# Window attention and AFNO over eight images: input and output turned by VectorE, the setup's loads and the plan's objective rewritten

## The chip, the cores and the metric

The kernel runs on one core of one Trainium2 chip. The core has TensorE (PE, with its weight loads listed apart as PEld), VectorE (DVE), ScalarE (ACT), GpSimd (POOL) and SyncE (SP), which here issues nearly all DMA transfers. The metric is the device time of one execution in microseconds (us); the number for the kernel before is the median of three runs. Everything is computed in float32, apart from one small bias product in bfloat16.

## The reference, cut

Two layers, one after the other, on an input of 8 images x 192 channels x 64 x 64. Layer 0 is window attention with the 16 largest scores kept in each row, and an MLP. Layer 1 is an AFNO (a Fourier transform, a tiny MLP on every frequency, the inverse transform) and an MLP.

```python
def _L0_conv_ref(x, ...):
    b, c, h, w = x.shape
    xs = jnp.transpose(x.reshape(b, c, h * w), (0, 2, 1))
    shortcut = _layer_norm(xs, norm1_g, norm1_b)
    ...
    qkv = (xin @ qkv_w.T + qkv_b).reshape(B_, N, 3, HEADS, HEAD_DIM)
    ...
    attn = jnp.einsum('bhnd,bhmd->bhnm', _l2n(q), _l2n(k)) * temperature
    kth = jax.lax.top_k(attn, IN_CC)[0][..., -1:]
    attn = jnp.where(attn >= kth, attn, NEG)
    rpb = jnp.transpose(rpb_table[REL_IDX], (2, 0, 1))
    attn = jax.nn.softmax(attn + rpb[None], axis=-1)
    out = jnp.einsum('bhnm,bhmd->bhnd', attn, v)
    ...
    out = out @ proj_w.T + proj_b
    ...
    x2 = shortcut + out
    hdn = _layer_norm(x2, norm2_g, norm2_b)
    hdn = jax.nn.gelu(hdn @ fc1_w.T + fc1_b, approximate=False) @ fc2_w.T + fc2_b
    x2 = x2 + hdn
    return jnp.transpose(x2, (0, 2, 1)).reshape(b, c, h, w)

def _L1_conv_ref(x, ...):
    skip1 = x
    xn = _layernorm(x.transpose(0, 2, 3, 1), n1_g, n1_b).transpose(0, 3, 1, 2)
    x = skip1 + _afno(xn, fc1_w, fc1_b, fc2_w, fc2_b)
    x_perm = x.transpose(0, 2, 3, 1)
    xn2 = _layernorm(x_perm, n2_g, n2_b)
    h = jax.nn.gelu(xn2 @ mlp1_w.T + mlp1_b, approximate=False) @ mlp2_w.T + mlp2_b
    return (h + x_perm).transpose(0, 3, 1, 2)
```

Here 192 channels, 6 heads of 32, MLPs of width 768. Both layers want tokens on the partitions for the norms and channels on the partitions for the products, so data is turned several times.

## The kernel before, in words

An image is cut into 8 bands of 8 rows (512 tokens, one row of windows), 64 bands in all. The work is written as generators, one for each task: `front(b, i)` loads and turns a band of image b, normalizes it and computes q, k and v; `attention(b, i, hb)` does half a band's windows; `back(b, i)` the projection and layer 0's MLP; `forward`, `pointwise` and `inverse` do the AFNO of an image in 12 groups of 16 channels; `leave(b, j)` does layer 1's MLP for a band and writes it out. AFNO needs all 8 bands of its image, so image b's AFNO and `leave` run beside attention of image b+1. Image 0 has nothing beside it, and image 7's last stages neither.

Before each piece of work a generator yields `op(engine, weight, ...)`: the engine (or a choice of two), an estimate of its time in units of about 10 ns, the buffers it takes and gives back (`get`, `put`), and what it waits for (`after`). `listed` (L96) collects these, and `Plan` (L130) plays them against each other: `run` (L215) places the ready piece that can begin first on an engine, ties decided by a key with the task's place in the program (`self.place`, 360 units an image); a buffer given back is free 15 units later (L268). `search` (L278) tries 80 noisy orders of the next 4000 units, keeps the one with the most work placed (PE's counts in full, other engines' 0.15), follows it for 2000 units and repeats. The kernel is then issued in that order, so every engine has a fixed instruction order. A piece on SP is a group of DMA issues, which SP works off in that order too, waiting at each for what it needs.

The parts that the change touches:

- Input. `load_band` (L377) brings a band in three transfers, channels on the partitions: 128 channels in rows of 2048 bytes (L381) and twice 64 channels in rows of 1024 bytes (L384). `front` turns it with six PE transposes into PSUM tile `lt` (L880, L884), ACT or DVE copies that to `xt` (L889). `loading` (L864) loads two bands ahead.
- Output. `leave` adds MLP and residual into `zt` (DVE, L1479), turns it with six PE transposes into `pz` (L1487), adds the MLP's second bias on ACT while it moves `pz` to `z` (L1491), and stores `z` with three transfers (L1494, L1496). `zt` is in an `xa` buffer, `z` in an `hn` buffer.
- The turn that other parts have already. In `mlp` with `by_dma` (L751) DVE turns blocks of 32 x 32 (L756, tile `lt_b` or `lt_d`, in an `att` buffer), four transfers write the blocks to DRAM rows (L765), three bring them back as channels (L768, L770, tile `hn_b` or `hn_d`). Attention's probabilities go likewise from image 1 on (`tt`, `ar`, `at`; L1069, L1078, L1081).
- Setup. `setup_layer1` (L606) loads AFNO's constants in one piece with the weight 0. Layer 1's gain `n1g` comes in eight transfers of single floats (L640), the MLP's weights `wmlp` right after it (L675). `setup_rows` (L518) spreads three vectors over the partitions through the tile `wides`.
- In attention each pair of rows of the top-16 search uses two of four `s2` buffers (L1138).

Of the kernel before, what the change touches and what calls it, by code (L numbers as in the profile page):

```python
# [9 lines left out]
FP = mybir.dt.float32  # L10
# [6 lines left out]
C = 192  # L17
# [112 lines left out]
class Plan:  # L130
# [84 lines left out]
    def run(self, until, noise=None):  # L215
        ops, clock, mode, units = self.ops, self.clock, self.mode, self.units
        at, front, place, ready = self.at, self.front, self.place, self.ready
        while ready:
# [48 lines left out]
            for name in put:  # L267
                units[name].append(end + (150 if engine == "sp" else 15))  # L268
                units[name].sort()
# [8 lines left out]
    def search(self, tries=80, step=2000, horizon=4000, spread=25):  # L278
        draw = random.Random(1)
        now = 0  # L280
        while self.ready:
            now = max(now, self.clock["pe"])
            kept, best = self.save(), None
            for k in range(tries):
                seed = draw.random()
                noise = drawn(seed, spread) if k else None
                if not self.run(now + horizon, noise):
                    self.restore(kept)
                    continue
                worth = 0  # L290
                for _, _, engine, begin, weight in self.log[kept[-1]:]:
                    part = min(weight, max(0, now + horizon - begin))
                    worth += part if engine == "pe" else 0.15 * part
                if not self.ready:
                    worth = 1e9 - max(self.clock.values())
                if best is None or worth > best[0]:
                    best = worth, seed if k else None
                self.restore(kept)
            seed = best[1]
            self.run(now + step, drawn(seed, spread) if seed is not None else None)  # L300
            now += step
        return [(self.names[task], engine, number) for number, task, engine, _, _ in self.log]

# [38 lines left out]
def program(ctx, tc, x, out, w):  # L342
# [34 lines left out]
    def load_band(b, i):  # L377
        xin = strip("xin", 2, f"xin_{b}_{i}")
        rows = x[b, :, 8 * i : 8 * i + 8, :]
        xa = xin[:, :BAND].rearrange("p (r s) -> p r s", s=HW)  # L380
        nc.sync.dma_start(xa, rows[0:CA])  # L381
        for t in range(2):
            xb = xin[64 * t : 64 * t + 64, BAND:ROW].rearrange("p (r s) -> p r s", s=HW)
            nc.sync.dma_start(xb, rows[CA:C, 4 * t : 4 * t + 4, :])  # L384
        xins[b, i] = xin

# [67 lines left out]
    wides = spare("wides", [128, 3, 2, 128])  # L454
# [20 lines left out]
    alongs = {name: ctile(name, [128, 2 * C]) for name in ("gain1", "bias1", "bias2")}  # L475
    gain1, bias1, bias2 = (
# [41 lines left out]
    def setup_rows():  # L518
# [17 lines left out]
        vectors = (vec(G1), pbias, vec(FC2B))  # L536
        yield op("dve", 150)
        for wide, v in zip((wides[:, i] for i in range(3)), vectors):
            for k, n in enumerate((CA, 64)):
                nc.vector.tensor_copy(wide[0:n, k, :], v[k][0:n].to_broadcast([n, 128]))  # L540
        yield op("pe", 60, "full", get="ps", put="h")
        pt = psum("along")
        for i in range(3):
            for k, n in enumerate((CA, 64)):
                to = pt[:, i // 2, i % 2 * C + k * CA : i % 2 * C + k * CA + n]
                nc.tensor.transpose(to, wides[0:n, i, k, :], ident[0:n, 0:n])
# [59 lines left out]
    def setup_layer1():  # L606
        yield op("pool", 0, get="xf", after=[("att", 0, 0, 1)])
# [9 lines left out]

# [3 lines left out]
        for k in range(4):  # L621
            src = w["fwd2"].rearrange("(a b k e) v -> k b a e v", a=2, k=4, e=2)[k]
            nc.sync.dma_start(frow[8 * k : 8 * k + 8], src)
        for c in range(1, 4):
            nc.sync.dma_start(frow[32 * c : 32 * c + 32], frow[0:32])
        inv1 = sb.tile([128, 128], FP, tag="xf", name="inv1", bufs=1)
# [6 lines left out]
        n1t = w["n1"]  # L633
        for c in range(2):
            for k in range(4):
                src = bass.AP(
                    n1t.tensor, n1t.offset + c * 2 * HC + k, [[0, 32], [4, 24], [1, 1]]
                )
                dst = n1g[32 * k : 32 * k + 32, 24 * c : 24 * c + 24]
                nc.sync.dma_start(dst.unsqueeze(2), src)  # L640
            nc.sync.dma_start(n1b2[:, c, :], w["n1"][c : c + 1, 1, :])
        yield op("dve", 120, after=[("att", 0, 1, 1)])
# [31 lines left out]
        nc.vector.tensor_scalar(n1b2, n1b2, float(HW), None, ALU.mult)  # L674
        wmlp.extend(load_mlp("wmlp1", "wmlp2"))  # L675
# [66 lines left out]

    def mlp(src, nm, w1, fc1_bias, w2, by_dma, then=None):
# [7 lines left out]
        if by_dma:  # L751
            ready = yield op("dve", 101, get="att rows", put="xa", after=last)
            turned = sb.tile([128, 6, 2, 2, 32], FP, tag="att", name=f"lt_{nm}", bufs=ATT_BUFS)
            whole = to.rearrange("p j (g k) -> p j g k", k=32)
            for t, g, c, n in ((0, 0, 0, 6), (1, 6, 4, 2), (1, 8, 0, 4)):
                nc.vector.transpose(  # L756
                    turned[:, c : c + n, t].rearrange("p g j k -> p j g k"),
                    whole[:, :, g : g + n],
                )
# [103 lines left out]

    def loading(b, i):  # L864
        yield op("sp", 154, get="xin", after=[], done=("xin", b, i))
        load_band(b, i)
# [3 lines left out]
    def front(b, i):  # L870
# [3 lines left out]
        yield op("pe", 66, "full", get="ps xt", put="xin", after=loaded)  # L874
        xin = xins.pop((b, i))
        pt = psum(f"lt_{nm}")
        for t, j in PAIRS:
            q = 2 * t + j
            c0 = t * (64 + C)
            nc.tensor.transpose(  # L880
                pt[:, j, c0 : c0 + CA], xin[:, q * 128 : (q + 1) * 128], ident
            )
        for j in range(2):
            nc.tensor.transpose(  # L884
                pt[:, j, CA : CA + 128], xin[:, BAND + j * 128 : BAND + (j + 1) * 128], ident
            )
        done = yield op(EITHER, (69, 87), put="ps")
        xt, pair = tokens("xt", XT_BUFS, f"xt_{nm}")
        copy(done, xt, pt[:, :, : 2 * C])  # L889
# [79 lines left out]
        def by_block(half, p):  # L969

            return half.rearrange("c (n b) -> c b n", b=2)[:, p]

        def qk_a(pq, p, first):
            for t in range(2):
                tok = by_block(xn[:, t * HALF : (t + 1) * HALF], p)
# [9 lines left out]
        def qk_b(pq, p, first):  # L985
            flags = dict(skip_group_check=True, stop=not first)
            for t in range(2):
                rows = slice(64 * t, 64 * t + 64)
                tok = by_block(xn[rows, BAND:ROW], p)
                nc.tensor.matmul(  # L990
                    pq[:, t, : 2 * C], tok, wqkv[1][rows, : 2 * C], start=first, **flags
                )
# [97 lines left out]
    def attention(b, i, hb):  # L1090
# [41 lines left out]
        for k0 in range(0, 12, 2):  # L1132
            yield op("dve", 90, get="sm" if k0 == 0 else "")
            if k0 == 0:
# [3 lines left out]
                sb.tile([128, 64], FP, tag="s2", name=f"s2_{nm}_{k0 + k}", bufs=4) for k in range(2)  # L1138
# [323 lines left out]
    def leave(b, j):  # L1462
# [3 lines left out]
        if j == 0:  # L1466
# [5 lines left out]
        xy = xys[b][0]  # L1472
        acc, last = yield from mlp(
            lambda t, q: xy[:, t, q, j, :], f"d{nm}", wmlp[0], fcb[:, 1, :], wmlp[1], True
        )
        left[b] -= 1
        yield op("dve", 88, get="xa", put="ps xy" if left[b] == 0 else "ps")
# [6 lines left out]
        )  # L1484
        yield op("pe", 66, "full", get="ps hn", put="xa")
# [29 lines left out]
        ([(setup_mlp(1, lambda: wmlp, *layer1, ["layer1", ("att", 0, 5, 1)]), 0.2)], 1),  # L1515
# [89 lines left out]
```

## Time and profile before

| What | Value |
|---|---|
| time, median of 3 runs | 4598.14 us (4592.67 to 4598.62) |
| the profiled run | 4606.84 us, its span 4605.0 us, mean granted TensorE clock 0.984 |
| share of the span busy: PE, PEld, DVE, ACT, POOL | 95, 75, 60, 54, 51% |
| DMA queue q1: packets, MB, share of 16 engines | 270414, 237.22, 18.6% |
| ACT `z<-pz` (L1491): 128x512 and 128x256, 64 each | 690 and 476 ns |
| ACT and DVE copies `xt<-lt` (L1041) | 46 of 803 ns and 18 of 943 ns |
| DVE transposes `lt_d<-xa_d` (L756), three shapes | 192, mean 415 ns |
| POOL bias add `xt<-xt,bias` (L1241) | 64 of 1869 ns |

A row of the profile names line, engine, operation and tiles (out<-in). Busy time is the union of an engine's instructions; matmuls overlap each other in PE's pipeline, so the sum of their lengths is more than PE's busy time. The idle time before an instruction is put down to what released it: "PE mh_d L807 <- DMA hn_d<-lr_d" says that PE stood still until that transfer had landed. An SP row is the time in which SP issues a transfer, not that in which the data moves. The durations all come from the one profiled execution.

### The profile page before, as it was taken

How to read it: one execution, taken by the hardware profiler on the slowest of the kernel's cores; microseconds unless marked ns; L12 is line 12 of the kernel's file. 1: busy time of each engine (PE TensorE's matmuls, PEld its weight loads, DVE VectorE, ACT ScalarE, POOL GpSimd, SP SyncE). 2: the span in 40 equal slices, each digit the busy share in tenths (PEclk: the TensorE clock that was granted, in tenths of full speed). 3: DMA queues.
4: the chain of work that ended last, by engine and by line, in shares of the span. 5: the costliest groups of instructions: out<-in, count | busy, mean ns of one | idle time of the engine just before them, and what ended most of it. 6: DMA issues, size and time to landing. Idle time of an engine off the chain costs nothing. (4 is left out here: it accounts for less than half of the span.)

```text
span 4605.0 us, 143865 instructions
## 1 busy us (share of the span) xinstructions
PE 4377.8 (95%) x60506; PEld 3470.0 (75%) x60506; DVE 2769.9 (60%) x11070; ACT 2506.5 (54%) x3693; POOL 2337.6 (51%) x2161
## 2 busy tenths in 40 slices
PE   7888999999999999999999999999999999999989
PEld 5777777887778777778767877778777787778758
DVE  7888776746774466763767456774576744742111
ACT  4555666545663456544656446564566544653552
POOL 7787765525564365652756246663375533631100
PEclk8999999999999999999999999999999999999999
DMA  2001221311123111221122211222112221111002
GB/s 55 16 12 50 57 60 41 98 52 43 50 57 94 49 47 47 67 73 50 47 56 63 71 50 54 57 64 71 56 47 57 74 63 43 47 47 52 19 19 66
DMA packets 271072, 246.42 MB, mean 54 GB/s; under 512 B 39983, under 2 KB 223482, under 8 KB 270426
## 3 DMA queue, kind: packets, MB, share of 16 engines
q1 hardware_dynamic: 270414, 237.22, 18.6%
q8 instruction: 476, 7.80, 0.7%
q14 instruction: 170, 1.39, 0.1%
q10 hardware_dynamic: 12, 0.00, 0.0%
HBM read 120.52 MB, written 116.39 MB: 51 GB/s over the span
## 5 line engine op out<-in xcount | busy, mean ns | idle before, releaser
L1349 ACT ACTIVATE fh<-fh,ab 128x1024 f32<-128x1024 f32 x768 | 814.1, 1113 | 374.3 <-PE fh L1366 372.0
L960 POOL TENSOR_TENSOR nrm<-nrm,mhalf 128x24 f32<-128x24 f32 x128 | 549.0, 4289 | 10.7
L853 PE MATMUL mo_b<-wfc,h_b 128*128 128x192 f32 x3072 | 529.1, 330 | 1.2 <-ACT fh L1349 1.0
L853 PE MATMUL mo_d<-wmlp,h_d 128*128 128x192 f32 x3072 | 514.2, 327 | 2.7 <-ACT h_d L791 2.6
L853 PEld LDWEIGHTS mo_b<-wfc,h_b 128*128 128x128 f32 x3072 | 502.4, 191 | 14.3 <-issue 6.9
L853 PEld LDWEIGHTS mo_d<-wmlp,h_d 128*128 128x128 f32 x3072 | 498.6, 190 | 11.3 <-ACT h_d L791 4.8
L1153 POOL TENSOR_TENSOR s<-s,top 128x768 f32<-128x768 f32 x128 | 193.7, 1514 | 602.9 <-DVE s L1150 452.3
L1366 PE MATMUL fh<-fz,w1p 32*128 32x264 f32 (+1 forms) x6144 | 454.5, 401 | 10.8 <-issue 2.9
L791 ACT ACTIVATE h_d<-mh_d,fcb 128x512 f32<-128x512 f32 x384 | 241.0, 686 | 286.3 <-PE mh_d L820 221.7
L1366 PEld LDWEIGHTS fh<-fz,w1p 32*128 32x128 f32 x6144 | 288.0, 184 | 144.0 <-issue 79.6
L1393 PE MATMUL fo<-fh,w2p 128*32 128x248 f32 (+1 forms) x6144 | 384.3, 385 | 9.3 <-issue 3.8
L807 PE MATMUL mh_b<-hn_b,wfc_a 128*128 128x256 f32 x1536 | 375.6, 390 | 15.7 <-DMA hn_b<-lr_b 5.7
L807 PE MATMUL mh_d<-hn_d,wmlp_a 128*128 128x256 f32 x1536 | 363.0, 386 | 18.8 <-DMA hn_d<-lr_d 16.8
L807 PEld LDWEIGHTS mh_d<-hn_d,wmlp_a 128*128 128x128 f32 x1536 | 284.5, 190 | 79.9 <-issue 39.4
L807 PEld LDWEIGHTS mh_b<-hn_b,wfc_a 128*128 128x128 f32 x1536 | 279.5, 190 | 85.2 <-issue 30.1
L1143 DVE MATCH_REPLACE8 s<-top,s 128x64 f32<-128x64 f32 x1536 | 309.8, 209 | 0.0
L1393 PEld LDWEIGHTS fo<-fh,w2p 128*32 128x32 f32 x6144 | 188.6, 110 | 154.1 <-issue 29.4
L1479 DVE TENSOR_TENSOR zt<-mo_d,xy 128x768 f32<-128x768 f32 x64 | 61.0, 952 | 396.9 <-PE mo_d L853 396.5
L1163 POOL TENSOR_TENSOR s<-s,rsum 128x768 f32<-128x768 f32 x128 | 192.6, 1508 | 207.3 <-DVE rsum L1161 159.2
L791 ACT ACTIVATE h_b<-mh_b,fcb 128x512 f32<-128x512 f32 x384 | 239.5, 692 | 86.5 <-PE mh_b L820 72.3
L1141 DVE MAX8 top<-s 128x8 f32<-128x64 f32 x1536 | 256.9, 209 | 42.1 <-ACT s L1041 41.3
L702 POOL TENSOR_SCALAR rs_d<-mv_d 128x4 f32<-128x4 f32 x64 | 14.6, 229 | 526.2 <-DVE mv_d L695 504.0
(213 smaller groups left out, 8716.9 us busy)
## 6 DMA issues: line engine op xcount, KB each, us to landing
ar<-tt SPq DMA_DIRECT2D x448, 96.0 KB
at<-ar SPq DMA_DIRECT2D x112, 384.0 KB
lr_d<-lt_d SPq DMA_DIRECT2D x256, 96.0 KB
lr_b<-lt_b SPq DMA_DIRECT2D x224, 96.0 KB
xin<-in_x SPq DMA_DIRECT2D x64, 256.0 KB
hn_d<-lr_d SPq DMA_DIRECT2D x64, 256.0 KB
out<-z SPq DMA_DIRECT2D x64, 256.0 KB
hn_b<-lr_b SPq DMA_DIRECT2D x56, 256.0 KB
```

The source lines that it names most:

```text
L791: nc.scalar.activation(to, of, AF.Gelu, bias=fc1_bias[:, 2 * fp + k : 2 * fp + k + 1],)
L807: nc.tensor.matmul(ph[:, t, k * HALF : (k + 1) * HALF], w1[0][:, f], hn[:, t * HALF : (t + 1) * HALF], start=(first and k == 0), stop=not ...
L853: nc.tensor.matmul(acc[:, j, t * C : (t + 1) * C], hs[f // 2][:, f % 2, q * 128 : (q + 1) * 128], w2[:, f, ORDER[t]], start=(f == 0 and t ...
L960: nc.gpsimd.tensor_tensor(nf, nf, mhalf[:, :24], ALU.pow)
L1141: nc.vector.max(best[:, 0:8], of)
L1143: nc.vector.match_replace(s2, best[:, 0:8], of, -3.0e38)
L1153: nc.gpsimd.tensor_tensor(s, s, top[:, :, :, 0:1].to_broadcast(shape), ALU.subtract)
L1163: nc.gpsimd.tensor_tensor(s, s, row(rsum), ALU.mult)
L1349: nc.scalar.activation(hs[hf, k], ph, AF.Gelu, bias=ab[:, 0:1])
L1366: nc.tensor.matmul(phs[k // 2][:, k % 2, cols], w1p[i][rows, hf].rearrange("p h v -> p (h v)"), fz[rows, :] if rhs is None else zu[rows, : ...
L1393: nc.tensor.matmul(po[rows, :] if i == 0 else pou[rows, :, 1 : U - 1], w2p[i][:, hf].rearrange("p a v -> p (a v)"), hs[hf, k // 2][:, k % ...
L1479: nc.vector.tensor_tensor(zt.rearrange("p j (t c) -> p j t c", t=2), acc[:, :, : 2 * C].rearrange("p j (t c) -> p j t c", t=2), xy[:, :, : ...
```

## The change

For images 1 to 7, `load_band` only takes the buffer, and `loading` issues 16 transfers in two pieces of eight, each of 32 partitions x 6 runs of 32 floats (`quarters`), so that blocks of 32 channels x 32 tokens lie ready in `xin`; `front` turns them with three DVE transposes straight into `xt`. Image 0 stays as it was. In `leave`, all but the last two bands of image 7 have the MLP's bias (`bias3`, spread over partitions by `setup_rows`) added to the residual by GpSimd beside the MLP, and `zt`, which now waits for that too, is turned by three DVE transposes into an `att` buffer and stored by 16 transfers in two pieces. `setup_layer1` is split into pieces on SP with weights, loads the gain by two broadcasts and sorts it with four DVE copies, and `wmlp` has a piece of its own. `s2` has two buffers instead of four. In the plan, a buffer comes back after the engine's own delay, and `search` makes 100 tries, counts PE's work by e to the power of 2 for each image that it lies behind the place reached (less for work ahead), other engines' by 0.05 of that, and can step back when no order goes on.

```diff
-                units[name].append(end + (150 if engine == "sp" else 15))
+                units[name].append(end + (150 if engine == "sp" else ARRIVES[engine]))
...
-    def search(self, tries=80, step=2000, horizon=4000, spread=25):
+    def search(self, tries=100, step=2000, horizon=4000, spread=25, mu=2.0, wt=0.05):
...
+            here = course[bisect.bisect(course, (done,))][1] if done < course[-1][0] else course[-1][1]
+            value = [math.exp(mu * (here - place) / 360) for place in self.place]
...
+                seed = draw.random() if k else None
+                if self.run(now + horizon, seed and drawn(seed, spread)):
+                    worth = 0
+                    for _, task, engine, begin, weight in self.log[kept[-1]:]:
+                        part = min(weight, max(0, now + horizon - begin)) * value[task]
+                        worth += part if engine == "pe" else wt * part
...
+            if best is None:
+                kept, now, done, counted = history[-min(3, len(history))]
+                del history[-3:]
+                self.restore(kept)
+                continue
+            history.append((kept, now, done, counted))
+            self.run(now + step, best[1] and drawn(best[1], spread))
...
     def load_band(b, i):
-        xin = strip("xin", 2, f"xin_{b}_{i}")
+        xin = xins[b, i] = strip("xin", 2, f"xin_{b}_{i}")
+        if b > 0:
+            return
...
-    wides = spare("wides", [128, 3, 2, 128])
+    wides = spare("wides", [128, 4, 2, 128])
...
-    alongs = {name: ctile(name, [128, 2 * C]) for name in ("gain1", "bias1", "bias2")}
...
+    alongs = {name: ctile(name, [128, 2 * C]) for name in ("gain1", "bias1", "bias2", "bias3")}
...
-        vectors = (vec(G1), pbias, vec(FC2B))
+        vectors = (vec(G1), pbias, vec(FC2B), vec(MLP2B))
...
     def setup_layer1():
-        yield op("pool", 0, get="xf", after=[("att", 0, 0, 1)])
+        yield op("sp", 420, get="xf", after=[("att", 0, 0, 1)])
...
+        yield op("sp", 280)
...
+        yield op("sp", 180)
...
+        yield op("sp", 280)
+        first = sb.tile([128, 128 + C], FP, tag="xf", name="first", bufs=1)
+        inv1, gains = first[:, 0:128], first[:, 128:]
...
-        n1t = w["n1"]
+        last = yield op("sp", 180)
         for c in range(2):
-            for k in range(4):
-                src = bass.AP(
-                    n1t.tensor, n1t.offset + c * 2 * HC + k, [[0, 32], [4, 24], [1, 1]]
-                )
-                dst = n1g[32 * k : 32 * k + 32, 24 * c : 24 * c + 24]
-                nc.sync.dma_start(dst.unsqueeze(2), src)
+            of = w["n1"][c, 0, :].partition_broadcast(128)
+            nc.sync.dma_start(gains[:, c * HC : (c + 1) * HC], of)
             nc.sync.dma_start(n1b2[:, c, :], w["n1"][c : c + 1, 1, :])
-        yield op("dve", 120, after=[("att", 0, 1, 1)])
+        yield op("dve", 60, after=[last])
+        for k in range(4):
+            rows = slice(32 * k, 32 * k + 32)
+            of = gains[rows].rearrange("p (n k) -> p k n", k=4)[:, k]
+            nc.vector.tensor_copy(n1g[rows], of)
...
+        yield op("sp", 200, done="wmlp")
         wmlp.extend(load_mlp("wmlp1", "wmlp2"))
...
+    PARTS = (0, 0, 0, 6), (1, 6, 4, 2), (1, 8, 0, 4)
...
+    def by_chunk(tile_):
+
+        blocks = tile_.rearrange("p j (g k) -> p j g k", k=32)
+        return [blocks[:, :, g : g + n] for _, g, _, n in PARTS]
...
+    def by_block(turned):
+
+        return [turned[:, c : c + n, t].rearrange("p g j k -> p j g k") for t, _, c, n in PARTS]
...
+    def quarters(tensor, b, i, half):
...
+        band = tensor[b, :, 8 * i : 8 * i + 8, :].rearrange("(g k) r s -> k g (r s)", k=32)
+        for a in (2 * half, 2 * half + 1):
+            for q in range(4):
+                yield band[:, :, 128 * q + 32 * a : 128 * q + 32 * a + 32], q, a
+
     def loading(b, i):
-        yield op("sp", 154, get="xin", after=[], done=("xin", b, i))
-        load_band(b, i)
+        if b == 0:
+            yield op("sp", 154, get="xin", after=[], done=("xin", b, i))
+            load_band(b, i)
+            return
+        for half in range(2):
+            name = ("xin", b, i) if half else None
+            yield op("sp", 368, get="" if half else "xin", after=[], done=name)
+            if half == 0:
+                load_band(b, i)
+            into = xins[b, i].rearrange("p (g q k) -> p q g k", q=4, k=32)
+            for of, q, a in quarters(x, b, i, half):
+                nc.sync.dma_start(into[32 * a : 32 * a + 32, q], of)
...
+        if b > 0:
+            yield op("dve", 101, get="xt", put="xin", after=loaded)
+            xt, pair = tokens("xt", XT_BUFS, f"xt_{nm}")
+            turned = xins.pop((b, i)).rearrange("p (g t j k) -> p g t j k", t=2, j=2, k=32)
+            for into, of in zip(by_chunk(xt), by_block(turned)):
+                nc.vector.transpose(into, of)
+        else:
...
-                sb.tile([128, 64], FP, tag="s2", name=f"s2_{nm}_{k0 + k}", bufs=4) for k in range(2)
+                sb.tile([128, 64], FP, tag="s2", name=f"s2_{nm}_{k0 + k}", bufs=2) for k in range(2)
...
+        turned_out = (b, j) < (B - 1, NB - 2)
...
+        def biased():
+            yield op("pool", 178, done=("biased d", b, j))
+            for t in range(2):
+                rows = xy[:, t, :, j, :]
+                nc.gpsimd.tensor_tensor(rows, rows, bias3[:, :, t * C : (t + 1) * C], ALU.add)
+
...
+        yield op(
...
+            put="ps xy" if left[b] == 0 else "ps",
+            after=[last, ("biased d", b, j)] if turned_out else None,
+        )
...
+        if turned_out:
+            yield op("dve", 101, get="att", put="xa")
+            turned = sb.tile([128, 6, 2, 2, 32], FP, tag="att", name=f"z_{nm}", bufs=ATT_BUFS)
+            for of, into in zip(by_chunk(zt), by_block(turned)):
+                nc.vector.transpose(into, of)
+            of = turned.rearrange("p g t j k -> p (t j) g k")
+            for half in range(2):
+                yield op("sp", 368, put="att" if half else "")
+                for into, q, a in quarters(out, b, j, half):
+                    nc.sync.dma_start(into, of[32 * a : 32 * a + 32, q])
+            return
...
-        ([(setup_mlp(1, lambda: wmlp, *layer1, ["layer1", ("att", 0, 5, 1)]), 0.2)], 1),
+        ([(setup_mlp(1, lambda: wmlp, *layer1, ["wmlp"]), 0.2)], 1),
```

## The prediction

> **What bounds it now.** I read the page's totals first, then busy time by stretch, then TensorE's waits, then stretches of the timeline. The page has TensorE (PE) busy for 95% of the span and no other engine over 60%.
>
> ```profile
> span 4605.0 us, 143865 instructions
> ...
> PE 4377.8 (95%) x60506; PEld 3470.0 (75%) x60506; DVE 2769.9 (60%) x11070; ACT 2506.5 (54%) x3693; POOL 2337.6 (51%) x2161
> ```
>
> The stretches are image 0 alone, the middle, and the tail after attention has ended. The columns are the stretch, its length, and busy time (count) of PE, PEld, DVE, ACT, POOL, then PE's granted clock, DMA share, GB/s.
>
> ```profile
> 0.00:460.00 460.00, 389.32 (x4718) 309.20 (x4718) 361.55 (x1578) 241.99 (x411) 349.82 (x304) 0.90 0.13 33
> 460.00:4300.00 3840.00, 3713.15 (x51996) 2944.59 (x51996) 2352.45 (x9322) 2126.45 (x3096) 1955.80 (x1811) 0.99 0.21 57
> 4300.00:4605.00 305.00, 275.28 (x3802) 216.21 (x3794) 55.86 (x171) 138.06 (x186) 31.96 (x46) 0.97 0.12 34
> ```
>
> PE is idle for 71, 127 and 30 us. Where the change works (460 to 4300) the idle share is 3.3%, so a PE instruction that goes is worth its slot in PE's queue, and a new wait of PE costs in full. Its present waits (total, times, longest):
>
> ```profile
> PE po L1186 <- DMA at<-ar: 29.0, 22, 2.7
> PE s L1113 <- DVE qkt L1103: 20.7, 13, 6.0
> ...
> PE mh_d L807 <- DMA hn_d<-lr_d: 16.8, 6, 13.6
> PE mh_b L807 <- DMA hn_b<-lr_b: 5.7, 4, 1.9
> ...
> PE pz L731 <- DVE zt L1479: 4.5, 6, 1.1
> ```
>
> DMA arrivals are the largest kind, 51.5 us, and all of these transfers pass SP's queue, which the change fills.
>
> **What goes from PE.** `front` loses the six transposes `lt` in images 1 to 7 (56 bands), `leave` the six `pz` in all but the last two bands (62): 118 groups. In the timeline (start, length) the slot is the distance to the next PE row, not the length:
>
> ```profile
> 2021.42 0.66 PE L731 MATMUL pz<-ident,zt 128*128 128x128 f32 x4
> ...
> 2021.91 0.38 PE L736 MATMUL pz<-ident,zt 128*128 128x128 f32 x2
> ...
> 2022.13 0.60 PE L731 MATMUL lc<-ident,xt 128*128 128x128 f32 x4
> ...
> 2029.73 1.10 DVE L756 STREAM_TRANSPOSE lt_d<-xa_d 128x384 f32<-128x384 f32 x3 [0.66 <-ACT xa_d L715]
> ...
> 2030.86 1.82 SPq L765 DMA_DIRECT2D lr_d<-lt_d  x4
> ```
>
> `pz` holds PE from 2021.42 to 2022.13, 0.71 us; two others (from 2032.89 and 4589.77) hold it 0.68. With 0.69: 118 x 0.69 = 81 us. The Trainium skill (TensorE: Matmul & The Clock Gate, Part 4: PE-mode transpose) gives some 275 ns for one 128x128 transpose in a kernel. The row agrees on the length (median 273 ns), but starts are 0.11 us apart, since transposes overlap. By the rule the gain would be 118 x 6 x 0.275 = 195 us; by the row it is 81, which I take. With them goes PE's wait for `zt`, 4.5 us: **-86 us on PE**.
>
> **The other engines.** ACT loses the two `z` activations (0.69 + 0.47 us, 62 times) and the `xt` copies it made (0.80 us, some 40): -104 us. DVE gains three transposes a group, the form of the `lt_d` row at 1.10 us: +130, less some 17 copies of 0.95: 2883 us, 64% of a shorter span. POOL gains `biased`, priced by the bias row L1241 at 1.87 us: +116, 2454 us. All of this lies beside PE. DVE sits idle 397 us before `zt` alone, so transposes after `zt` fit; without that cover the cost would be the 113 us of DVE. In `front`, 1.10 us on DVE replaces 0.69 on PE and 0.80 on ACT, no longer chain.
>
> `zt` now also waits for `biased`. Behind it on DVE stand attention's MAX8 and the next statistics, and PE waits for these. But POOL adds the bias right after `ms_d` and the reads of `xy` that normalize (for which L1241 waited 74.3 us in 64, so 72 us more of POOL in 62), and PE then has 12 to 20 us of the MLP before `zt` can start; POOL's queue waited 504 us for DVE before `rs_d`, so it isn't behind. On POOL, attention's two passes over the scores come 3 us later. Cost nothing, 188 us if POOL were full. The stored tile takes one of five `att` buffers for about 10 us (16 issues of 0.455 and the landing), 0.13 buffer on average, and frees an `hn` buffer, for which SP waited 15.3 us. The two `s2` buffers are used by DVE alone, in order, and MATCH_REPLACE8 has no idle before it: nothing.
>
> **SP and DMA** decide. A band's load and its store become 16 transfers each of 192 runs of 128 bytes instead of 3. The nearest row for the issue is `lr_d`: also 192 runs (of 512 bytes), 1.82 us for four, 0.455 each. SP's band before is 2 x (1.82 + 1.43) for the MLPs, 2 x (1.79 + 0.34) for attention, 1.43 + 1.51 for input and output: 13.7 us of 72. After it is 13.7 - 2.9 + 32 x 0.455 = 25.4 us, 36%. An urgent transfer (`lr`, `hn`, `ar`, `at`: eight a band) meets a busy SP some 16% more often and then waits half of a burst of eight, 1.8 us: 0.16 x 1.8 x 8 x 56 = 129 us of delay in all, of which PE sees little, as most of it is in the plan. I take a twelfth, **+10 us**.
>
> What a run of 128 bytes costs the engines no row shows for this pattern. From below: the packet records have the 256 packets of 132 bytes of `fhalf` (read in order) passing in 0.5 us, 31 ns on each of 16 engines, so 12 x 31 = 0.37 us a transfer, less than its issue. From above: the tiny `n1g` transfers held SP itself:
>
> ```profile
> 80.80 16.05 SPq L640 DMA_DIRECT2D n1g<-in_n  x4
> ...
> 97.38 2.72 SPq L381 DMA_DIRECT2D xin<-in_x  x1
> ```
>
> Four transfers of 768 runs of 4 bytes took 16.05 us: 16.05 x 16 / 3072 = 84 ns. The Trainium skill (DMA: Bandwidth & Descriptors, Specifications and Rules for kernel authors) speaks against the change: line rate needs 512 bytes, below that the engine reads, modifies and writes, and transfers under 64 KB pay mostly overhead. The rows agree on the overhead (a quarter of the bytes at the same 0.455 us), but SP pays it off the path. I take 31 to 45 ns, since 132 bytes is near 128 and 4 is not; the upper end is the rival below.
>
> **Setup and plan.** `n1g` becomes two broadcast loads and four copies on DVE; SP gets 20 us back near 73 to 97 us. PE waited for an input only once, 3.8 us for the first, and the AFNO first uses `n1g` at 396 us: nothing, and nothing lost if the loads move later by 100 us. `bias3` adds two small transposes and some DVE copies in the first 30 us: under 2 us. The new plan (a buffer comes back 28 instead of 15 units after PE, work behind its place weighs more) has no row. From below, half of the 127 us of idle in the middle could go (-60); from above, the same could come (+60). The idle share is already small and the known errors (SP time of the setup, late buffers) are mended, so I take -15.
>
> Sum: 4605 - 86 + 10 - 15 = 4514 us of span. The profiled run lasted 4606.84 us, 8.7 over the median of 4598.14, so against the median: 4598 - 91 = **4507 us**.
>
> **Rivals.** (1) *The plan gains more*: half the idle in the middle goes. For it: 71 + 127 us lie idle, and fewer `ps` slots are taken (each `lt` or `pz` held one some 2.4 us). Against: the waits are scattered, none over 29 us in total. 4598 - 86 + 10 - 62 = 4460. (2) *Another engine takes the slot back*: PE has less to do in a band, but attention's chain over DVE and POOL doesn't shrink, and DVE gains 113 us. For it: DVE's slices of 7 and 8 tenths. Against: PE waits for DVE only some 40 us now. A gain of a third: 4598 - 30 = 4568. (3) *Slower*: the 128-byte runs drain at the 84 ns of `n1g`. A burst of eight then holds SP 8.1 us, not 3.64, four bursts a band, and `at` and `hn` behind it come 4.4 us later than planned. About 236 bursts, a quarter of that excess seen by PE: 236 x 1.1 = 260 us; 4598 - 91 + 260 = 4767. It decides from a third of that, an excess of 1.5 us a burst, near 53 ns a run. For it: scattered runs to and from DRAM, and the input after `n1g` issued in 10.7 us instead of 1.4. Against: `lr` and `ar`, 1280 runs issued in 3.7 us, stayed at the pace of their issue. That the transposes don't leave PE is excluded by the code.
>
> **Chances.** Forecast 0.52 (own range 4470 to 4545), rival 1 0.22, rival 2 0.14, rival 3 0.12. About 0.2% (9 us) is what a measurement of this kernel tells from no change. Rival 2 gives 0.04 to "same" and 0.01 to "slower": faster 0.83, same 0.04, slower 0.13. The range 4430 to 4590 leaves out rival 3 and the far end of rival 1.
>
> **What would show it.** Right: no `pz` rows beyond two bands, PE's busy sum down by 80 to 90 us, idle near 228 us, `xin` and `out` at 0.45 us an issue, the three DMA waits of PE under 75 us together. Wrong: issues of `xin` or `out` of 0.7 us and more, or PE's waits for `at` or `hn` above 130 us (rival 3); PE's idle up by 50 with DVE as the releaser (rival 2); PE's idle down by 50 (rival 1).

## The result, and the profile after

The changed kernel takes 4513.03 us (median of 4 runs, 4509.2 to 4528.45), the kernel before 4595.94 us in 4 runs (4592.67 to 4598.62). The ratio is 0.9824, with an interval of 0.9803 to 0.9845: some 81 us less, by the ratio. The forecast of 4507 us was 6 us too low. The experiments below show larger errors in three of its terms, which cancel: that it came so near is luck.

The page of the changed kernel, its first lines and that of the DMA queue (packets, MB, share of 16 engines):

```profile
span 4512.5 us, 144599 instructions
...
PE 4272.9 (95%) x59800; PEld 3397.5 (75%) x59800; DVE 2878.6 (64%) x11399; ACT 2430.3 (54%) x3553; POOL 2465.8 (55%) x2291
...
q1 hardware_dynamic: 621262, 237.40, 22.3%
```

The span is 92.5 us shorter. PE is busy for 104.9 us less, and idle for 239.7 us where it was 227.2 (span less busy time): all of the gain is busy time of PE, and idle time took 12.5 us of it back. (The profiled execution of the kernel before took 4606.84 us, over all its other times, so differences between its profile and others come out up to some 10 us larger than those between medians.) The bytes are the same in 2.3 times the packets.

The same three stretches by engine, with the columns of the table before:

```profile
0.00:460.00 460.00, 381.79 (x4494) 300.78 (x4495) 352.73 (x1533) 241.97 (x411) 341.81 (x294) 0.89 0.14 32
460.00:4200.00 3740.00, 3612.45 (x51336) 2881.90 (x51338) 2460.41 (x9670) 2050.93 (x2967) 2077.85 (x1938) 0.99 0.25 59
4200.00:4513.00 313.00, 278.62 (x3980) 214.83 (x3972) 65.43 (x197) 137.39 (x177) 46.20 (x60) 0.97 0.14 33
```

The idle times are 78, 128 and 34 us. The middle is 100 us shorter and still has the 127 us of idle it had before; it is there that the time went.

PE's waits (total, times, longest):

```profile
PE po L1249 <- DMA at<-ar: 30.0, 22, 4.1
PE mh_d L844 <- DMA hn_d<-lr_d: 25.6, 10, 12.8
PE s L1176 <- DVE qkt L1166: 21.5, 8, 7.0
...
PE mh_b L844 <- DMA hn_b<-lr_b: 2.8, 3, 1.7
```

The three DMA waits come to 58.4 us, 51.5 before. By this view the 16 transfers cost PE 7 us. SP's own timeline (start, length, transfers) shows what that view does not:

```profile
2001.53 1.76 SPq L1141 DMA_DIRECT2D ar<-tt  x4
2003.34 4.91 SPq L1577 DMA_DIRECT2D out<-z  x8
2008.30 0.44 SPq L1144 DMA_DIRECT2D at<-ar  x1
2008.78 3.93 SPq L1577 DMA_DIRECT2D out<-z  x8
2012.81 1.88 SPq L802 DMA_DIRECT2D lr_d<-lt_d  x4
```

`ar` writes attention's turned probabilities to DRAM, and `at`, which attention needs, brings them back once `ar` has landed. Eight issues of a store stand in front of `at`, and another eight in front of `lr_d`.

### The profile page after: what moved, and what is told of

The parts are those of the page before. It is cut to its first block, busy times and chain, and to the rows that moved or that the text cites. A ratio compares the mean times of both kernels' runs of the same rounds, so it can differ in the third digit from the quotient of the medians.

```text
span 4512.5 us, 144599 instructions
## 1 busy us (share of the span) xinstructions
PE 4272.9 (95%) x59800; PEld 3397.5 (75%) x59800; DVE 2878.6 (64%) x11399; ACT 2430.3 (54%) x3553; POOL 2465.8 (55%) x2291
## 3 DMA queue, kind: packets, MB, share of 16 engines
q1 hardware_dynamic: 621262, 237.40, 22.3%
## 4 chain that ended last, share of the span: by engine, by line
PE 33%; DVE 6%; POOL 4%; DMA 2%; ACT 2%; SPq 2%; issue 2%; DVEq 0%; ACTq 0%; POOLq 0%
PE mo_d L890 5%; PE mo_b L890 4%; PE fh L1429 4%; PE mh_d L844 4%; PE fo L1456 3%; PE mh_b L844 2%; PE mh_d L857 2%; POOL nrm L1023 1%; PE mh_b L857 1%; PE fy L1504 1%; PE pq L1039 1%; DMA at<-ar 1%; DVE s L1206 1%; PE fa L1359 1%; PE fb L1477 1%
## 5 line engine op out<-in xcount | busy, mean ns | idle before, releaser
L890 PEld LDWEIGHTS mo_b<-wfc,h_b 128*128 128x128 f32 x3072 | 504.6, 192 | 19.1 <-issue 12.5
L1456 PE MATMUL fo<-fh,w2p 128*32 128x264 f32 (+1 forms) x6144 | 380.1, 384 | 6.3 <-ACT fh L1412 3.7
L844 PEld LDWEIGHTS mh_d<-hn_d,wmlp_a 128*128 128x128 f32 x1536 | 287.0, 192 | 89.5 <-issue 47.3
L1204 DVE MAX8 top<-s 128x8 f32<-128x64 f32 x1536 | 255.5, 207 | 38.7 <-ACT s L1104 38.4
L1208 DVE MAX8 top<-s 128x8 f32<-128x64 f32 x1536 | 265.3, 214 | 0.0
L1104 ACT COPY fo<-fo 128x264 f32<-128x264 f32 x187 | 70.7, 378 | 333.2 <-PE fo L1456 332.9
```

The lines of the kernel that those rows point to most:

```text
L844: nc.tensor.matmul(ph[:, t, k * HALF : (k + 1) * HALF], w1[0][:, f], hn[:, t * HALF : (t + 1) * HALF], start=(first and k == 0), stop=not ...
L890: nc.tensor.matmul(acc[:, j, t * C : (t + 1) * C], hs[f // 2][:, f % 2, q * 128 : (q + 1) * 128], w2[:, f, ORDER[t]], start=(f == 0 and t ...
L1204: nc.vector.max(best[:, 0:8], of)
L1208: nc.vector.max(best[:, 8:16], s2)
L1456: nc.tensor.matmul(po[rows, :] if i == 0 else pou[rows, :, 1 : U - 1], w2p[i][:, hf].rearrange("p a v -> p (a v)"), hs[hf, k // 2][:, k % ...
```

## The experiments

All times are set against the kernel before as run on the same chip for that comparison, 4592 to 4594 us.

### The three parts alone

**The turns alone** (input and output by DVE, GpSimd's bias; with two `s2` buffers; the old search, delay of buffers and setup's loads left as they were, apart from `bias3`):

```diff
     def load_band(b, i):
-        xin = strip("xin", 2, f"xin_{b}_{i}")
+        xin = xins[b, i] = strip("xin", 2, f"xin_{b}_{i}")
+        if b > 0:
+            return
...
+        if turned_out:
+            yield op("dve", 101, get="att", put="xa")
```

> The turns by VectorE alone, with the old plan search and the old setup. Theory of the prediction (PE's slots are what is saved): 75 to 95 us under the kernel before, so about 4505 to 4520, PE busy down by about 100 us as in the whole change. Rival (the plan is the gain, the freed slots turn into new waits): less than 30 us under before, 4565 or more, with PE's busy time down by as much and its idle time up by 60 us or more.

Measured: 4561.74 us, ratio 0.9938 (0.9926 to 0.9951), 31 us faster. Its page:

```profile
span 4559.5 us, 144562 instructions
...
PE 4308.7 (94%) x59800; PEld 3405.6 (75%) x59800; DVE 2882.8 (63%) x11441; ACT 2394.8 (53%) x3491; POOL 2463.5 (54%) x2289
```

PE ran exactly as many instructions as in the changed kernel, was busy for 69 us less than before, and idle for 24 us more (250.8). The gain lies at the edge of the rival's range, but idle time grew by 24 us and not by 60: part of the slots came back as waits, and PE's busy time fell by less than the 100 us expected.

**The plan alone** (the first three parts of the diff on the kernel before):

```diff
-                units[name].append(end + (150 if engine == "sp" else 15))
+                units[name].append(end + (150 if engine == "sp" else ARRIVES[engine]))
...
-    def search(self, tries=80, step=2000, horizon=4000, spread=25):
+    def search(self, tries=100, step=2000, horizon=4000, spread=25, mu=2.0, wt=0.05):
```

> The new plan search and the new delay of returned buffers alone; PE still turns input and output, the setup is the old one. Theory of the prediction: within 20 us of the kernel before (4575 to 4615), PE's busy time unchanged. Rival (the plan is the gain): 50 us or more under before, 4545 or less, all of it out of PE's idle time.

Measured: 4550.81 us, ratio 0.9908 (0.9893 to 0.9923), 42 us faster. Its page:

```profile
span 4560.6 us, 143927 instructions
...
PE 4346.1 (95%) x60506; PEld 3462.8 (76%) x60506; DVE 2773.3 (61%) x11078; ACT 2497.0 (55%) x3684; POOL 2330.2 (51%) x2158
```

The same 60506 PE instructions as before keep PE busy for 32 us less, and idle for 13 us less. So the theory missed, and so did the rival's "all of it out of idle time". The three DMA waits are 36.7 us, not 51.5:

```profile
PE mh_d L830 <- DMA hn_d<-lr_d: 19.2, 5, 13.6
...
PE po L1209 <- DMA at<-ar: 15.7, 18, 2.3
...
PE mh_b L830 <- DMA hn_b<-lr_b: 1.8, 4, 0.6
```

**The setup alone** (`setup_layer1` in pieces on SP with weights, the gain by broadcasts, `wmlp` by itself):

```diff
-        yield op("pool", 0, get="xf", after=[("att", 0, 0, 1)])
+        yield op("sp", 420, get="xf", after=[("att", 0, 0, 1)])
```

> The replanned setup alone, in the kernel before. Theory of the prediction: no input was waited for, so nothing beyond what any new order of the plan moves, within 15 us of before; SP's 22 us on the small gain loads are gone. Rival (the setup held up image 0): 15 us or more under before, all within the first 460 us.

Measured: 4627.1 us, ratio 1.0078 (1.0065 to 1.009), 34 us slower. Both expectations missed. In the first 460 us, where the loads are, PE idles 71.7 us against 70.7 before, so no idle time was gained there. But the order of the whole kernel is another as well, since the search's course depends on every weight. The next comparisons ask how much that alone can do.

### How much an order is worth

The plan draws its noise from a fixed start of the random numbers. Another start changes nothing but the order of the work.

```diff
-        draw = random.Random(1)
+        draw = random.Random(2)
```

The changed kernel, the kernel before, the turns alone and the plan alone with start 2, and the kernel before with start 3:

> The whole change with another seed of the plan's random search. Theory now: the order that the search happens to find moves the time by 10 to 25 us either way, so 4490 to 4540. Rival: the order hardly matters, within 5 us of the changed kernel, and the three parts interact in another way.

> The kernel before with another seed. Theory now: within 10 to 25 us of before on either side, which would make the 34 us that the setup alone cost, and part of the 42 us of the plan alone, luck of the order. Rival: within 5 us of before; then the setup alone really costs.

> The turns alone (old search, old setup) with another seed. Theory now: PE's freed 90 us less some 31 us for the 16 transfers give about 58 us on average over orders, so 4520 to 4560, and the first order's 31 us was on the bad side. Rival: again near 4562, then the turns are worth 31 us with the old plan whatever the order.

> The new plan search and buffer delays alone (PE turns, old setup), with the second seed. Theory now: the new search is worth some 50 us on an average order and is steadier than the old one, so about 4550 again (4535 to 4570) although the old search with this seed gave 4666; the turns then are worth 4551 to 4513 and about 4550 to 4489, that is 40 to 60 us. Rival (the gain of the new search on the first seed was luck of the order): over 4590.

> The kernel before with a third seed. Theory now: the order of before is one of the lucky ones of the old search, whose orders scatter by some tens of us, so this lies between the first two, 4610 to 4660. Rival (the second seed was an odd one out): within 12 us of before, 4581 to 4605.

Measured, the medians in us by the start of the random numbers:

| | old search | new search |
|---|---|---|
| turned on PE | 4593 (1), 4665.6 (2), 4621.91 (3) | 4550.81 (1), 4559.85 (2) |
| turned on DVE | 4561.74 (1), 4542.33 (2) | 4513.03 (1), 4489.19 (2) |

The kernel before moved further with its start than expected (73 us, not 10 to 25); the other four came within their ranges or 1 us beside them. The ratios to the kernel before are 1.0157 (1.014 to 1.0174) for its own start 2, 1.0067 (1.0051 to 1.0084) for its start 3; 0.9888 (0.9874 to 0.9903) for the turns and 0.9922 (0.9899 to 0.9946) for the plan with start 2; and 0.9768 (0.9753 to 0.9783) for the changed kernel with start 2. The right lower cell has the new setup with it, the left lower one has not.

By the old search the same kernel spans 73 us over three starts; the order of the kernel before is the best of the three. By the new search the two pairs lie 9 and 24 us apart. The mean over starts 1 and 2 falls from 4629 to 4552 by the turns, to 4555 by the plan and to 4501 by both: 77, 74 and 128 us. With start 1 alone these were 31, 42 and 80. A single pair of orders thus doesn't measure a part of this kernel to better than some tens of us. In particular the 34 us of the setup are within what another order does by itself, and what the setup is worth stays open. That the turns and the plan both gain is well supported all the same: each does so in all four of its comparisons in the table (the turns 31 to 123 us, the plan 42 to 106).

### The PE slots in a fixed order

To free the slots and change nothing else, the order of the kernel before was kept, without the 118 groups of six PE transposes; the copies that followed them read `xin` and `zt` instead.

```diff
-        for t, j in PAIRS:
+        turned = b == 0
+        for t, j in PAIRS if turned else ():
...
-        copy(done, xt, pt[:, :, : 2 * C])
+        copy(done, xt, pt[:, :, : 2 * C] if turned else xin.rearrange("p (j n) -> p j n", j=2))
...
-        to_channels(pz, pair, zt)
+        turned = (b, j) >= (B - 1, NB - 2)
+        if turned:
+            to_channels(pz, pair, zt)
```

> The kernel before in its own order of instructions, but without the 118 groups of PE transposes that the change takes away: the copy to xt reads xin itself, the bias of the output reads zt itself. This leaves out the turning of input and output for these bands. Nothing else moves, no DMA is added. Theory of the prediction: PE's busy time falls by about 90 us and the time by 80 to 95, since a slot of PE is worth its length. Rival (a fixed order turns freed slots into waits for others): PE's busy time falls as much, but the time by less than 50 us, and PE's idle time grows.

Measured: 4572.46 us, ratio 0.995 (0.9934 to 0.9965), 20 us faster. Its page and PE's waits:

```profile
span 4574.5 us, 142409 instructions
...
PE 4309.2 (94%) x59798; PEld 3402.9 (74%) x59798; DVE 2764.1 (60%) x11070; ACT 2507.2 (55%) x3693; POOL 2341.7 (51%) x2161
```

```profile
PE po L1187 <- DMA at<-ar: 31.0, 23, 4.3
...
PE fa L1297 <- POOL xf L1291: 11.7, 13, 2.1
...
PE s L1114 <- issue: 8.6, 5, 2.1
...
PE po L1187 <- ACT fh L1350: 4.1, 5, 1.3
```

Counted from one PE start to the next, the groups' rows fall from 97.7 to 8.2 us, 89.5 us or 0.76 a group: the slot was sized well. But PE's busy sum falls by 69 only, since its other groups took 21 us more; a granted clock of 0.981 instead of 0.984 would make 13 of these (an estimate: 0.3% of 4378). And its idle time rises by 38, from 227 to 265 us. No one wait took it. Rows of the kernel before to set beside these:

```profile
PE fa L1296 <- POOL xf L1290: 7.2, 9, 1.8
...
PE po L1186 <- ACT fh L1349: 0.5, 1, 0.5
```

Summed over all of PE's waits, those for ACT grew by 17 us, for DVE and "issue" by 7 each, for POOL by 4, for DMA by 3. The likely reading is that in a fixed order PE arrives earlier at operands that arrive when they did; the rows fit this and do not prove it. Part of the shortfall goes with the clock: the four executions without the transposes took 4564.47 us at a granted clock of 0.984 and 4576.51 at 0.981, and the kernel before had 0.984 to 0.987. At an equal clock the gain would be some 30 us (an estimate from that slope of 4 us for 0.001), still about a third of the 89.5.

### What the 16 transfers cost

The same order again, that of the changed kernel: each piece of eight transfers on SP keeps its place, and issues one and two long ones in place of its eight; for input and output, and for the output alone. The bytes moved are the same; what is left out is their right arrangement. The edit of the output, which the two kernels share:

```diff
-                for into, q, a in quarters(out, b, j, half):
-                    nc.sync.dma_start(into, of[32 * a : 32 * a + 32, q])
+                if half == 0:
+                    to = rows[0:CA]
+                    nc.sync.dma_start(to, of[:, 0:BAND].rearrange("p (r s) -> p r s", s=HW))
+                    continue
+                for t in range(2):
+                    nc.sync.dma_start(
+                        rows[CA:C, 4 * t : 4 * t + 4, :],
+                        of[64 * t : 64 * t + 64, BAND:ROW].rearrange("p (r s) -> p r s", s=HW),
+                    )
```

> The whole change in its own order of instructions, but each band's input and output goes in 3 transfers with long runs instead of 16 with runs of 128 bytes. This leaves out the right arrangement of input and output: the data is in the wrong place. Theory of the prediction: the 16 transfers cost 10 us, so this is 5 to 15 us under the changed kernel. Rival (the short runs eat much of the gain): 30 us or more under the changed kernel, PE's waits for at and hn nearly gone. Other rival (nothing is seen of them): within 5 us.

> The changed kernel in its own order, the input still in 16 transfers a band, but the output in 3 long ones. This leaves out the right arrangement of the output. Theory: what costs is SP held by bursts, and input and output issue about the same number, so half of the 31 us comes back: 12 to 20 us under the changed kernel. Rival (short writes to DRAM are the dear ones): 25 us or more. Other rival (short reads are): under 8 us.

Measured: 4481.74 us for both (ratio 0.9758, 0.9744 to 0.9771) and 4482.1 us for the output alone (0.9761, 0.9741 to 0.9781), 31 us less than the changed kernel each. So the short transfers cost 31 us, three times the term of the prediction, and the output's have nearly all of it: the expected half missed, and the size is that of the rival by which short writes are the dear ones. The page and PE's waits with the output in long transfers:

```profile
span 4477.8 us, 143637 instructions
...
PE 4263.9 (95%) x59800; PEld 3396.8 (76%) x59800; DVE 2873.6 (64%) x11399; ACT 2429.6 (54%) x3553; POOL 2467.1 (55%) x2291
```

```profile
PE mh_d L844 <- DMA hn_d<-lr_d: 16.6, 4, 13.2
...
PE po L1249 <- DMA at<-ar: 12.5, 15, 2.2
...
PE mh_b L844 <- DMA hn_b<-lr_b: 2.3, 2, 1.7
```

The three DMA waits fall from 58.4 to 31.4 us, by 27.0, and all idle of PE by 25.8 (239.7 to 213.9). So the cost is these waits, and the profile after alone could not show it: 58.4 us looked like the 51.5 of before, while without the bursts this plan would have had 31.4. With input and output in long transfers the waits are 29.2 us, and PE idles 209.6:

```profile
span 4479.3 us, 142867 instructions
...
PE 4269.7 (95%) x59800; PEld 3396.2 (76%) x59800; DVE 2876.4 (64%) x11399; ACT 2429.1 (54%) x3553; POOL 2467.5 (55%) x2291
```

```profile
PE mh_d L844 <- DMA hn_d<-lr_d: 14.7, 2, 12.8
PE po L1254 <- DMA at<-ar: 14.5, 12, 3.3
```

The SP rows tell why mostly the output. The issues of input and output are about equally long (`xin` 0.52 us, `out` 0.49 us on average), so the writes are not dearer to issue. But of 100 unbroken bursts of stores in the changed kernel 59 stand directly in front of an urgent transfer (`lr`, `hn`, `ar`, `at`), of 86 bursts of loads 26. From DVE's last turn to the first issue `lr_d` takes 1.48 us on average, 0.16 with long stores and 0.39 before; from the last `ar` to `at` it is 2.96, 2.33 and 2.11.

Summed over all `lr`, `hn`, `ar` and `at`, the time from the work or the issue that each follows to its own first issue is 844 us in the changed kernel, 614 with long stores and 537 with long loads too. The short stores thus delay urgent transfers by 230 us in all, the short loads by 77, and PE's idle time tells of 26 and 4 us of that. The place in SP's queue fits both numbers roughly. That a short write itself also lands later is not excluded, since these profiles have no landing times. DVE waited for a stored tile's buffer only 0.2 us, so the `att` buffers are not the cause. Why the plan puts stores in front of urgent work more often than loads was not tried.

### Smaller bursts

The version that follows from this: four pieces of four transfers for input and output, so that urgent transfers can be planned between them; each piece with a weight of 2.05 us, and start 8.

```diff
-        draw = random.Random(1)
+        draw = random.Random(8)
...
-        for a in (2 * half, 2 * half + 1):
-            for q in range(4):
-                yield band[:, :, 128 * q + 32 * a : 128 * q + 32 * a + 32], q, a
+        a = half
+        for q in range(4):
+            yield band[:, :, 128 * q + 32 * a : 128 * q + 32 * a + 32], q, a
...
-            for half in range(2):
-                yield op("sp", 368, put="att" if half else "")
+            for half in range(4):
+                yield op("sp", 205, put="att" if half == 3 else "")
```

> The changed kernel with each band's input and output in four pieces of four transfers on SP instead of two of eight, at the measured weight of 205 units a piece (0.51 us an issue), and another seed, so a new order. Theory (the bursts delay urgent transfers behind them): the gain of smaller pieces is up to half of the 31 us, within the scatter of orders: 4465 to 4505, PE's waits for at and hn under 45 us together. Rival (the number of issues costs, not the length of a piece): 4490 to 4530, these waits still 50 us or more.

Measured: 4475.83 us, ratio 0.9746 (0.9724 to 0.9767), the fastest of all that were run, 37 us below the changed kernel. Its page and PE's waits:

```profile
span 4471.8 us, 144666 instructions
...
PE 4263.7 (95%) x59800; PEld 3384.2 (76%) x59800; DVE 2856.4 (64%) x11374; ACT 2412.2 (54%) x3561; POOL 2454.0 (55%) x2282
```

```profile
PE po L1249 <- DMA at<-ar: 24.5, 20, 3.4
PE mh_d L844 <- DMA hn_d<-lr_d: 18.7, 9, 12.9
...
PE mh_b L844 <- DMA hn_b<-lr_b: 8.2, 5, 3.4
```

The time is as expected, the reason only in part. Stores that stand right in front of urgent transfers hold SP for 198 us in all, not 311. But the three waits are 51.4 us, where under 45 was expected and the changed kernel has 58.4: 7 us of the 31.6 by which PE's idle fell. The rest is spread, and PE's busy sum is 9 us lower. The start was changed with the pieces, and the changed kernel with start 2 has 212 us of idle too (it took 4489.19 us). The granted clock differs as well: 0.986 in all four executions, 0.978 to 0.981 in those of the changed kernel. So how much of the 37 us the smaller bursts make was not separated from order and clock.

## Why the prediction was right, and where it was not

**The total: right.** 4507 forecast, 4513.03 measured, well in the range. Three of its terms were not, and they cancel by luck. Of the signs named, PE's busy sum fell by 105 us, not 80 to 90, and idle stood at 240 us, not near 228.

**The slots of PE, -86 us: the count right, the worth wrong.** The rows give 89.5 us in place of 81 and the wait. The step that failed is "a PE instruction that goes is worth its slot in PE's queue". An idle share of 3.3% says that PE seldom waits with its present load; it does not say how far ahead of PE the operands are. In the fixed order a quarter is gained (20 us; about a third at an equal clock). As far as these runs can tell, most of the slots became time only with an order made anew around the shorter PE work. By the new search, with stores in long transfers, the whole change is worth 111 us, the plan alone 42: the difference of 69 us is near the 86 (with the setup in it, and within the scatter of orders).

**SP and DMA, +10 us: right in kind, a third of the size.** SP's issues went from 939 to 1652 us, 37% of the span, as worked out, and an issue lasts 0.5 us, not the 0.7 and more of the slow rival. What was mis-sized is the delay of the urgent transfers: 129 us forecast, 308 measured against the same order with long transfers. The sum let them meet a busy SP by chance, 16% more often; the plan puts 59 bursts of stores right in front of them. The "twelfth" that reaches PE was near: 31 of 308 is a tenth. The sign named for this step, three waits under 75 us together, came out (58.4) and proved nothing, since it was held against the waits of the old order. The rule of the Trainium skill that was weighed (DMA: Bandwidth & Descriptors, Specifications: at least 512 bytes for line rate) is not what cost time here: with the input in long or in short runs the time is 4481.7 or 4482.1 us. The packet records agree with it in direction: a run of 128 bytes took an engine 12.5 ns on average, one of 512 bytes 31, which is more for each byte of the short ones.

**The plan, -15 us: too small.** With start 1 it is -42 us by itself, within the bounds of 60 that were set; with start 2, -106. The reason "the known errors are mended" looked only at idle time, of which the plan alone takes 13 us. The larger part with start 1 is busy time, 32 us with the same instructions, which the prediction held fixed.

**The other engines: right.** DVE has 2878.6 us of busy time (2883 forecast), POOL 2465.8 (2454) and ACT 2430.3 (2402; it took 140 instructions less, 24 fewer than reckoned). The turns of output and input last as reckoned, 127.8 us on DVE for 118 groups; the bias was sized at 1.87 us a band and takes twice 1.02:

```profile
L1572 DVE STREAM_TRANSPOSE z<-zt 128x384 f32<-128x384 f32 x186 | 67.8, 415 | 1.9
...
L935 DVE STREAM_TRANSPOSE xt<-xin 128x384 f32<-128x384 f32 x168 | 60.0, 407 | 0.0
...
L1542 POOL TENSOR_TENSOR xy<-xy,bias 128x384 f32<-128x384 f32 x124 | 124.5, 1024 | 29.6 <-ACT xa_d L743 21.6 <-DVE xa_d L748 8.0
```

These are rows of groups (times, busy, mean ns, idle before). DVE waits 1.9 us before turning the output and none before the input, and its idle before `zt` is 241 us where it was 397: the cover was there and is not used up.

**Setup, nothing: agrees where it can be seen** (71.7 us of idle in the first stretch for 70.7); as a whole it stays open, as said.

**The rivals.** The slow one is excluded by the issue times. "Another engine takes the slot back" was right about what happens in the fixed order, though it is not one engine, and wrong about the changed kernel, to which a new order came as well; PE's waits for DVE, put at "some 40 us" there, are 51 us when all rows are added. "The plan gains more" named about the right size for the plan (62 us; 42 and 106 measured), but not where it came from: by the plan alone idle fell by 13 us only, and in the changed kernel it rose.

Put together, with terms as measured: -20 for the slots in the old order, about -91 more by the new order with less work for it on PE, +31 for the stores, -80 us in all. The middle number is what remains, -80 + 20 - 31, and is not a measurement of its own.

## What to carry to other kernels

Where a planner fixes every engine's order, price a change in the order it will get, not in the present one: removing 90 us of PE work in place gave 20. The same kernel in other orders differed by 73 us, so judge a part by several orders before a few tens of us are believed. Before splitting a store into many transfers, look at what stands behind it in the queue that issues it; cheap issues in a block of eight delayed the turns that PE was waiting for, and this cost shows against the same order with long transfers, not against the waits of the old kernel.

## What was not expected of the hardware

PE's busy time is no constant of its instructions. With the same 60506 of them it was 4377.8 us in the kernel before, 4346.1 by the new search and 4391.2 by the old one with start 2: up to 45 us, or 1%, at granted clocks of 0.983 and 0.984. The six kernels with these instructions fall into two groups. The two planned by the new search have 3238 and 3250 stretches in which PE stays at one line and tile, and 4346 and 4353 us of busy time; the four by the old search have 3296 to 3318 stretches and 4375 to 4391 us. Whether the changes from one group of instructions to another are the cause was not tried.

The granted clock goes with the order too. In one comparison on one chip the medians were 0.985 for the kernel before, 0.981 for the turns alone and 0.9855 for the plan alone. Why was not tried.

The 128-byte runs were no burden on the DMA engines: they raised the queue's share of the 16 engines from 18.6 to 22.3% of the span. In 41 unbroken bursts of over 1000 such runs a run drained every 23 to 47 ns on an engine (1536 runs in 2.40 us are 25 ns on each of 16). The issues alone set a pace of 41 ns (eight of 0.49 us for 1536 runs), so the runs themselves cost no more than the fastest bursts show, and less than the 31 to 45 ns of the prediction.
